# A plan that chooses the engine of low parts and last sums, finer records of Q and K, and column tiles for layer 2 and V in a macaron block

## The chip, the cores and the metric

The kernel runs on one core of one Trainium2 chip. The metric is device time in microseconds (us) of one execution; the time before is the median of three runs. A core has TensorE (PE; its weight loads are shown apart as PEld), VectorE (DVE), ScalarE (ACT), GpSimd (POOL) and SyncE (SP, which here issues most DMAs). They run side by side and meet through semaphores. Every engine takes its own instructions strictly in the order in which the program lists them, so the order in which the kernel is written down decides what waits for what.

## What is computed

A macaron block on x of 32 x 256 x 128 (32 sequences of 256 tokens, width 128): half a feed-forward network, attention, half a feed-forward network, each with a norm in front. The weights of the network are booleans that mean +1 or -1.

```python
def ffn(x, k0, k1, k2, s0, s1, s2):           # 256 -> 512 -> 512 -> 128
    h = concatenate([x, -x], axis=-1)
    h = relu(s0 * (h @ where(k0, 1, -1))) * 2
    h = relu(s1 * (h @ where(k1, 1, -1))) * 2
    return s2 * (h @ where(k2, 1, -1))

def attn(x, Wq, bq, Wk, bk, Wv, bv, gamma, beta):   # 16 heads of 8
    Q, K, V = (heads(x @ W.T + b) for W, b in ((Wq, bq), (Wk, bk), (Wv, bv)))
    a = softmax(einsum('bhqd,bhkd->bhqk', Q, K) / sqrt(8), axis=-1)
    return layernorm(merge(einsum('bhqk,bhkd->bhqd', a, V)) + x, gamma, beta)

x = x + 0.5 * ffn(layernorm(x), ...)
x = x + attn(layernorm(x), ...)
x = x + 0.5 * ffn(layernorm(x), ...)
```

## The kernel before

**Tiling.** Two sequences make a unit: 16 units of 512 tokens, and each unit has two halves (one sequence each) in the attention. Values are split into a high and a low half-precision part, so that two or three half-precision matmuls stand for one in single precision.

**Stages of a unit.** `first(u)` is the first feed-forward network: `normalize` (statistics on DVE, the rest on POOL, or all on DVE where `quick` is set), `turned` (a transpose by DMA from ACT's and POOL's high and low parts, or on PE where `quick` is set), then `ffn`. In `ffn`, layer 0 makes four tiles `p` of 128 x 512, layer 1 four more of eight matmul steps each; `relu_split` takes each tile out of PSUM as a high part (ACT, line 556, `h1h` or `h2h`) and a low part (DVE, line 562, `h1l` or `h2l`). For a hand-picked tile (`SOFT`: the second tile of layer 1) ACT writes the rectified tile a second time (line 559, `full`) and POOL subtracts (line 560). Layer 2 (line 606) makes four groups of 128 tokens, eight steps of 128 columns each. The last sum `x + factor * p` runs on DVE (line 618) for units 0, 1 and 15, and on ACT and POOL (lines 615 and 616) for the others. `norm_attn` and `project` make Q, K and V: `qkhl` (lines 670 and 672), a DMA to DRAM (line 675), and three row DMAs each that lay Q and K out by heads (line 680); V (line 689) is copied into `vaug`. `maxima` computes the scores `nat` once (line 720) for the row maxima `nm` (DVE, line 731); `shift` turns the maxima into extra rows of Q (`mt` at lines 741 and 742, a transpose `pm` at line 748, `mr` at line 753, DMAs at lines 754 and 755); `weigh` computes the scores again (`sc`, line 788), exponentials on ACT (`pt`, line 800) and the context `cx` (line 770). `context` copies and transposes it (`cxT` at line 803, `tp` at line 814), divides (lines 833 and 834), normalizes and adds (lines 836 to 841; on POOL, or on DVE where `quick` is set). `second(u, b)` is the second network; for unit 15 it runs by halves.

**The plan.** Nothing is emitted where it is written. Each `op(...)` notes engine, assumed cost, rank, what it reads and writes, and the buffers it holds. `simulate` then plays the program with these costs: an engine that is free takes the ready operation of lowest rank whose buffers fit; PE may pass over a group that is not ready, within `SKIP` ranks. The order found in this way is the order in which `run` emits each engine's instructions. Scores of the two kinds with the same rank (`kind` "M" and "W") go out interleaved, as they use different row tiles. A unit has 16 ranks; `B0`, `BA`, `BP`, `BW`, `BV` and `B1` shift the stages against one another: the weights of a half come `BW` = 11 ranks after its maxima. `QF` and `QK` say how many first units use the quick norm and PE transposes.

**Tile forms of PE.** A step of `dense` can use the full array ("D", 128*128 in the profile) or four column tiles ("C", 128*32: four weight loads and four matmuls). Scores use row tiles ("R", 32*128), the context column tiles. An operation of kind "F" takes the form that PE is in; after scores it takes the next one in line. Layer 2 and V were always "D", with ranks rounded (`even`) so that they come together.

Of the kernel before, what the change touches and what calls it, by code (L numbers as in the profile page):

```python
# [35 lines left out]
F32 = mybir.dt.float32  # L36
# [7 lines left out]
P = 128  # L44
# [12 lines left out]
QF, QK = 2, 2  # L57

SOFT, SOFT_FIRST, FIRST = ((1, 1),), ((1, 1),), 2
# [5 lines left out]
B0, BA, BP, BW, BV, B1 = -34, -12.911, -7.641, 11, 3, 41.956  # L65

RUSH, AHEAD = 0, 5.808

SKIP0, SKIP, UNTIL = 21.758, 7.907, 11.451

WAIT = 0.087

TURN, DRAIN, SIGNAL = 0.105, 0.22, 0.06

SAME = (0.0, 0.09, 0.09, 0.1, 0.0)
# [18 lines left out]
class _Node:  # L94
    __slots__ = ("n", "eng", "cost", "emit", "rank", "kind", "rows", "lag", "needs", "then", "bufs", "count", "avail", "start", "given", "tiling")


class _Plan:
# [11 lines left out]
    def op(self, eng, cost, emit, r=(), w=(), rank=0.0, kind="D", rows=0, lag=None):  # L110
        x = _Node()
        x.n, x.eng, x.cost, x.emit, x.rank, x.kind, x.rows = len(self.nodes), eng, cost, emit, rank, kind, rows
        x.lag = lag if lag is not None else DRAIN if eng == PE else SIGNAL
        x.then, x.avail, x.start, x.given = [], 0.0, None, lag is not None
# [25 lines left out]
    def simulate(self):  # L140
# [17 lines left out]

        def tiling(x):
            return "R" if x.kind in "WM" else x.tiling if x.kind == "F" else x.kind  # L160

        def begin(group, now):
# [11 lines left out]
            for x in group:  # L174
# [3 lines left out]
                for b in x.bufs:  # L178
# [4 lines left out]
                    if not b.left:  # L183
                        tick += 1
                        heapq.heappush(events, (now + span + x.lag, tick, b.tag))
                for y in x.then:
                    y.avail = max(y.avail, now + span + (x.lag if y.eng != eng or x.given else SAME[eng]))
# [52 lines left out]

        mode = "D"
        while left:
# [8 lines left out]
            while again:  # L251
                again = False
                for eng in range(5):
                    if free[eng] > now + 1e-9 or not ready[eng]:
                        continue
                    if eng == PE:
                        group = choose(now)
                    else:
                        can = [x for x in ready[eng] if x.avail <= now + 1e-9 and fits(x)]
                        group = [min(can, key=lambda x: (x.rank, x.n))] if can else None  # L260
# [31 lines left out]
def tile_macaron(ctx: ExitStack, tc: tile.TileContext, x, Wq, bq, Wk, bk, Wv, bv, gamma, beta, k0, k1, k2, s0, s1, s2, out):  # L292
# [176 lines left out]
    def blanks():  # L469
        for j in range(NV):  # L470
            rank = -500 if j == 0 else (j - 1) * UNIT * 0.5
            op(POOL, 1.35, lambda j=j: nc.gpsimd.memset(vaug[j], 0.0), w=[("V", j)], rank=rank)
            op(POOL, 0.95, lambda j=j: nc.gpsimd.memset(ks[j].bitcast(I32), ONES), w=[("K", j)], rank=rank)
# [9 lines left out]
    def normalize(dst, src, tag, n, rank, scale=1.0, quick=False):  # L483
# [7 lines left out]
        for a in range(0, n, step):  # L491
            part = slice(a, a + step)
            ts = range(a, a + step)
            for t in ts:
# [4 lines left out]
               r=[(mv, t) for t in ts], w=[(ve, a)], rank=rank, lag=0.12)  # L499
            op(POOL, 0.25 + 0.2 * step, lambda part=part: nc.gpsimd.tensor_tensor(rs.t[:, part, 0], ve.t[:, part], nhalf[:, part], ALU.pow),  # L500
               r=[(ve, a), "nhalf"], w=[(rs, a)], rank=rank, lag=0.15)
# [52 lines left out]
    def relu_split(hi, lo, m, ps, w, rank, soft):  # L554

        op(ACT, 0.09 + w / 1280, lambda: nc.scalar.activation(hi.t[:, m, :], ps.t, AF.Relu), r=[ps], w=[(hi, m)], rank=rank)  # L556
        if soft:
            full = buf(work, [P, w], F32, "full", 2, "full")
            op(ACT, 0.09 + w / 1280, lambda: nc.scalar.activation(full.t, ps.t, AF.Relu), r=[ps], w=[full], rank=rank)
            op(POOL, 0.1 + w / 500, lambda: nc.gpsimd.tensor_tensor(lo.t[:, m, :], full.t, hi.t[:, m, :], ALU.subtract), r=[full, (hi, m)], w=[(lo, m)], rank=rank)  # L560
        else:
            op(DVE, 0.08 + w / 985, lambda: nc.vector.scalar_tensor_tensor(lo.t[:, m, :], ps.t, 0.0, hi.t[:, m, :], ALU.max, ALU.subtract),  # L562
               r=[ps, (hi, m)], w=[(lo, m)], rank=rank)

    def ffn(key, srcs, dst, n, rank, span):
# [4 lines left out]
        softs = SOFT_FIRST if key[1] < FIRST and key[0] == "ffn0" else SOFT  # L570

        at = lambda i: rank + span * i / (NF + NF * NF + n)
        even = lambda k: 2 * (k // 2) + 0.9
# [4 lines left out]
        for m in range(NF):  # L578
# [7 lines left out]
            relu_split(*h1, m, ph, w, at(i), (0, m) in softs)  # L586
            i += 1
        for m in range(NF):
# [9 lines left out]
            relu_split(*h2, m, ph, w, at(i), (1, m) in softs)  # L598
        po = psum([P, n, D], f"p3{name}")
        h2s = [(h, m) for h in h2 for m in range(NF)]  # L600
        for t in range(n):

            def layer2(t=t):
                for c in range(NF):
                    for k in range(2):
                        nc.tensor.matmul(po.t[:, t, :], h2[k].t[:, c, bass.ts(t, P)], w2[:, c, :], start=c == 0 and k == 0, stop=c == NF - 1 and k == 1)  # L606

            op(PE, 0.449, layer2, r=[*h2s, "w2"], w=[po], rank=even(at(i)))
# [5 lines left out]
        if 1 < key[1] < NU - 1:  # L614
# [281 lines left out]
```

## Time and profile before

| | us |
|---|---|
| median of three runs (708.55 to 709.5) | 708.56 |
| the profiled execution | 707.94 |
| its span, from the first to the last instruction | 706.1 |
| first row maximum starts | 54.86 |
| last row maximum ends | 658.7 |
| last exponential ends | 675.4 |

A profile shows one execution. A row of the timeline gives the start, the length, the engine, the line, the operation, and the tile written and those read; `x4` means four of them merged into one row, and a bracket at the end says how long the engine had stood idle and who ended it. A row of the waits names who waited for whom, then the total in us, how often, and the longest. A row of the groups ends in the busy time, the mean length in ns and the idle time in front. Matmuls overlap, so the distance from one start to the next tells more of PE than the length of one.

### The profile page before, as it was taken

What the parts mean: (1) busy time and instruction counts of PE and PEld (TensorE: products, weight loads), DVE (VectorE), ACT (ScalarE), POOL (GpSimd) and SP (SyncE); (2) the same over time, 40 slices, a digit from 0 to 9 for tenths busy, and PEclk for the clock granted to TensorE, in tenths of its full rate; (3) what the DMA queues carried; (4) which work ended last, traced back from release to release, by engine and by line L of the source; (5) the groups of instructions that cost most, each with busy time, mean ns of one, the idle gap of its engine ahead of it and who ended that gap; (6) DMA issues with size and microseconds to landing.
All of it is one profiled execution on the core that took longest, in us unless ns stands there. A gap on an engine that the chain in (4) does not pass through costs nothing.

```text
span 706.1 us, 23287 instructions
## 1 busy us (share of the span) xinstructions
PE 652.2 (92%) x9800; PEld 331.8 (47%) x9800; DVE 601.4 (85%) x1229; ACT 527.0 (75%) x770; POOL 445.8 (63%) x579
## 2 busy tenths in 40 slices
PE   2996888999999999999999999999999998989797
PEld 1553343445454454545545454545555454444336
DVE  7789888999989889898989989898988898978564
ACT  3552777878788787888888877888878777867853
POOL 7762647668492877749586956858582928463611
PEclk9998999999999999999999999999999999999989
DMA  5141331422213132232323131332232030410100
GB/s 138 31 120 62 63 107 27 107 42 85 64 33 117 33 108 56 67 81 48 101 44 120 34 108 42 93 56 72 62 48 86 19 117 19 108 33 4 33 1 32
DMA packets 79373, 46.28 MB, mean 66 GB/s; under 512 B 50562, under 2 KB 74628, under 8 KB 79268
## 3 DMA queue, kind: packets, MB, share of 16 engines
q1 hardware_dynamic: 77796, 44.20, 24.7%
q8 instruction: 77, 1.26, 0.7%
q10 hardware_dynamic: 1472, 0.59, 0.3%
q14 instruction: 28, 0.23, 0.1%
HBM read 20.25 MB, written 13.24 MB: 47 GB/s over the span
## 4 chain that ended last, share of the span: by engine, by line
PE 70%; DVE 17%; ACT 6%; issue 3%; DMA 3%; POOL 0%; SPq 0%; ACTq 0%; DVEq 0%; POOLq 0%
PE cx L770 14%; PE p_None L325 12%; PE p L325 9%; PE p L322 7%; PE sc L788 6%; DVE nm L731 6%; PE p L606 4%; ACT pt L800 4%; PE nat L720 3%; PE p_None L606 3%; PE p_None L322 3%; DVE h1l L562 3%; PE tp L814 2%; DMA dm<-mr 1%; PE pq L325 1%
## 5 line engine op out<-in xcount | busy, mean ns | idle before, releaser
L731 DVE TENSOR_REDUCE nm<-nat 128x4 f32<-128x1024 f32 x256 | 310.7, 1217 | 46.9 <-PE nat L720 38.0
L800 ACT ACTIVATE pt<-sc,esc 128x1024 f32<-128x1024 f32 x256 | 284.9, 1116 | 79.7 <-PE nat L720 41.0
L770 PE MATMUL cx<-pt,vaug 128*32 128x256 f32 x2048 | 147.6, 389 | 2.3 <-ACT pt L800 2.3
L325 PEld LDWEIGHTS <-w 128*32 128x32 f16 x3584 | 91.6, 96 | 92.2 <-issue 32.7
L788 PE MATMUL sc<-Q,ks 32*128 32x256 f16 x1024 | 103.6, 275 | 11.0 <-ACT pt L800 8.0
L720 PE MATMUL nat<-ks,Q 32*128 32x256 f16 x1024 | 101.5, 275 | 8.1 <-ACT pt L800 4.1
L770 PEld LDWEIGHTS cx<-pt,vaug 128*32 128x32 f32 x2048 | 64.9, 111 | 54.9 <-issue 16.4
L325 PE MATMUL p_None<-h1h_None,w 128*32 128x512 f16 x780 | 77.4, 382 | 0.2 <-DVE h1l_None L562 0.2
L325 PE MATMUL p_None<-h1l_None,w 128*32 128x512 f16 x780 | 76.8, 379 | 0.0
L325 PE MATMUL p<-h1h,w 128*32 128x512 f16 x644 | 66.2, 383 | 0.4
L788 PEld LDWEIGHTS <-ks 32*128 32x128 f16 x1024 | 31.7, 93 | 73.1 <-issue 64.6
L325 PE MATMUL p<-h1l,w 128*32 128x512 f16 x644 | 65.9, 381 | 0.0
L616 POOL TENSOR_TENSOR x<-x,x 128x512 f32<-128x512 f32 x13 | 16.6, 1279 | 64.8 <-ACT x L615 64.8
L322 PEld LDWEIGHTS <-w 128*128 128x128 f16 x424 | 38.7, 98 | 36.7 <-issue 9.1
L556 ACT ACTIVATE h2h<-p 128x512 f16<-128x512 f32 (+1 forms) x72 | 41.2, 572 | 17.9 <-PE p L322 14.3
L836 POOL TENSOR_TENSOR y<-y,axn 128x256 f32<-128x256 f32 x30 | 21.8, 728 | 49.9 <-DVE y L834 41.3
L556 ACT ACTIVATE h1h<-p 128x512 f16<-128x512 f32 (+1 forms) x72 | 39.4, 571 | 18.2 <-PE p L325 11.1
L720 PEld LDWEIGHTS <-Q 32*128 32x128 f16 x1024 | 31.4, 92 | 38.3 <-issue 35.9
L562 DVE SCALAR_TENSOR_TENSOR h1l<-p,h1h 128x512 f16<-128x512 f32 (+1 forms) x72 | 45.7, 650 | 3.2 <-ACT h1h L556 2.7
L562 DVE SCALAR_TENSOR_TENSOR h2l<-p,h2h 128x512 f16<-128x512 f32 (+1 forms) x54 | 35.3, 653 | 12.0 <-ACT h2h L556 11.8
L562 DVE SCALAR_TENSOR_TENSOR h1l_None<-p_None,h1h_None 128x512 f16<-128x512 f32 x60 | 39.5, 682 | 6.8 <-ACT h1h_None L556 6.6
L322 PE MATMUL p<-h1h,w 128*128 128x512 f16 (+1 forms) x127 | 43.4, 354 | 1.3 <-DVE h1l L562 0.8
(144 smaller groups left out, 1368.4 us busy)
## 6 DMA issues: line engine op xcount, KB each, us to landing
dr<-qkhl SPq DMA_DIRECT2D x32, 256.0 KB
Q<-dr SPq DMA_DIRECT2D x48, 128.0 KB
ks<-dr SPq DMA_DIRECT2D x48, 128.0 KB
x<-in_L_attn_x_dram SPq DMA_DIRECT2D x15, 256.0 KB
out_dram<-x_None SPq DMA_DIRECT2D x15, 256.0 KB
Q<-nought SPq DMA_DIRECT2D x16, 128.0 KB
dm<-mr SPq DMA_DIRECT2D x32, 16.0 KB
Q<-dm SPq DMA_DIRECT2D x32, 16.0 KB
```

What stands on the lines that cost most here:

```text
L322: nc.tensor.matmul(to, w, of, start=start, stop=stop)
L325: nc.tensor.matmul(to[32 * r : 32 * r + 32], w[:, 32 * r : 32 * r + 32], of, start=start, stop=stop)
L556: op(ACT, 0.09 + w / 1280, lambda: nc.scalar.activation(hi.t[:, m, :], ps.t, AF.Relu), r=[ps], w=[(hi, m)], rank=rank)
L562: op(DVE, 0.08 + w / 985, lambda: nc.vector.scalar_tensor_tensor(lo.t[:, m, :], ps.t, 0.0, hi.t[:, m, :], ALU.max, ALU.subtract), r=[ps, ( ...
L606: nc.tensor.matmul(po.t[:, t, :], h2[k].t[:, c, bass.ts(t, P)], w2[:, c, :], start=c == 0 and k == 0, stop=c == NF - 1 and k == 1)
L616: op(POOL, 1.23, lambda: nc.gpsimd.tensor_tensor(dst.t, dst.t, of(), ALU.add), r=reads, w=dsts, rank=at(i))
L720: nc.tensor.matmul(nat.t[:, ii, qc, :], Q.t[32 * r : 32 * r + 32, g, b * S + qc * P : b * S + qc * P + P], K[32 * r : 32 * r + 32, g, b * ...
L731: op(DVE, 1.141, lambda g=g, pr=pr, nat=nat: nc.vector.tensor_reduce(nm.t[:, :, 2 * pr : 2 * pr + 2, g].rearrange("p q i -> p i q"), nat.t ...
L770: nc.tensor.matmul(cx.t[32 * r : 32 * r + 32, g // 2, :], V[:, 2 * b + kc, 4 * (g // 2) + r, 16 * (g % 2) : 16 * (g % 2) + 32], pts[g, r / ...
L788: nc.tensor.matmul(sc.t[:, ii, kc, :], K[32 * r : 32 * r + 32, g, b * S + kc * P : b * S + kc * P + P], Q.t[32 * r : 32 * r + 32, g, b * S ...
L800: op(ACT, 1.012, lambda pt=pt, sc=sc: nc.scalar.activation(pt.t, sc.t, AF.Exp, scale=esc), r=[sc, "esc"], w=[pt], rank=rank - RUSH)
L836: op(e, cost, lambda: eng.tensor_tensor(y.t, y.t, xn.t[:, 2 * b : 2 * b + 2, :], ALU.add), r=[(xn, 2 * b), (xn, 2 * b + 1)], w=[(y, 0)], r ...
```

## The change

- Constants: `QF`, `QK` 2 to 1; a new `QL` = 2; `BW` 11 to 13, `BV` 3 to 4, the other offsets by less than one rank; `RUSH` 0 to 0.302; `SKIP0` 21.758 to 30.226. The hand-picked `SOFT` tiles are gone.
- Lags: the time from an operation's end to its reader's start is now noted by the pair of engines (`AFTER`, `REACH`).
- `relief`: when ACT is free, the plan looks at DVE's ready operations that have an alternative (`alt`: every low part and every last sum). If the detour over ACT and POOL would end no later than `BIAS` after DVE's own end, a new ACT operation is made, and the old one moves to POOL.
- Layer 2 and V become kind "F", and use `dense` and so column tiles where PE is in that form.
- The rows of Q and K are noted apart, so that the plan lets the three row DMAs of one tile overlap.
- The last `QL` units use the quick context and the quick norm of the second network.

```diff
-QF, QK = 2, 2
-
-SOFT, SOFT_FIRST, FIRST = ((1, 1),), ((1, 1),), 2
+QF, QK = 1, 1
+
+QL = 2
...
-B0, BA, BP, BW, BV, B1 = -34, -12.911, -7.641, 11, 3, 41.956
-
-RUSH, AHEAD = 0, 5.808
-
-SKIP0, SKIP, UNTIL = 21.758, 7.907, 11.451
-
-WAIT = 0.087
-
-TURN, DRAIN, SIGNAL = 0.105, 0.22, 0.06
-
-SAME = (0.0, 0.09, 0.09, 0.1, 0.0)
+B0, BA, BP, BW, BV, B1 = -34, -12.145, -7.563, 13, 4, 42.5
+
+RUSH, AHEAD = 0.302, 5.298
+
+SKIP0, SKIP, UNTIL = 30.226, 7.856, 12.452
+
+WAIT = 0.101
+
+KIND2 = 'F'
+
+TURN = 0.1
+
+
+AFTER, REACH = (0.165, 0.085, 0.11, 0.04, 0.0), (0.053, 0.033, 0.037, 0.08, 0.05)
+
+BIAS = 0.471
...
+        def until(x, eng):
+            return x.lag if x.lag is not None else 0.0 if x.eng == eng == PE else AFTER[x.eng] + REACH[eng]
...
+        def relief(now, best):
+
+            nonlocal left
+            for x in sorted((x for x in ready[DVE] if x.alt and x.avail <= now + 1e-9), key=lambda x: (x.rank, x.n)):
+                if best and (best.rank, best.n) < (x.rank, x.n):
+                    return None
+                act, evict, source, temp, pool, rest = x.alt
+                before = sum(y.cost for y in ready[DVE] if y.avail <= now + x.cost and (y.rank, y.n) < (x.rank, x.n))
+                wait = sum(y.cost for y in ready[POOL] if (y.rank, y.n) < (x.rank, x.n))
+                other = max(now + act + 0.2, max(free[POOL], now) + wait) + pool
+                if other > max(free[DVE], now) + before + x.cost + BIAS:
+                    continue
...
+                x.eng, x.cost, x.emit, x.count, x.alt = POOL, pool, rest, 1, None
+                ready[ACT].append(y)
+                left += 1
+                return y
+            return None
...
-                        group = [min(can, key=lambda x: (x.rank, x.n))] if can else None
+                        best = min(can, key=lambda x: (x.rank, x.n)) if can else None
+                        if eng == ACT:
+                            best = relief(now, best) or best
+                        group = [best] if best else None
...
-    def relu_split(hi, lo, m, ps, w, rank, soft):
+    def relu_split(hi, lo, m, ps, w, rank):
...
-        if soft:
...
+        op(DVE, 0.08 + w / 985, lambda: nc.vector.scalar_tensor_tensor(lo.t[:, m, :], ps.t, 0.0, hi.t[:, m, :], ALU.max, ALU.subtract),
+           r=[ps, (hi, m)], w=[(lo, m)], rank=rank,
+           alt=(0.09 + w / 1280, lambda: nc.scalar.activation(full.t, ps.t, AF.Relu), ps, full, 0.1 + w / 500, low(full)))
...
-                        nc.tensor.matmul(po.t[:, t, :], h2[k].t[:, c, bass.ts(t, P)], w2[:, c, :], start=c == 0 and k == 0, stop=c == NF - 1 and k == 1)
-
-            op(PE, 0.449, layer2, r=[*h2s, "w2"], w=[po], rank=even(at(i)))
+                        dense(po.t[:, t, :], h2[k].t[:, c, bass.ts(t, P)], w2[:, c, :], tiling, c == 0 and k == 0, c == NF - 1 and k == 1)
+
+            op(PE, 0.449, layer2, r=[*h2s, "w2"], w=[po], rank=LAYER2(at(i)), kind=KIND2)
...
-        if 1 < key[1] < NU - 1:
-            op(ACT, 0.586, lambda: nc.scalar.activation(dst.t, po.t, AF.Identity, scale=fac), r=[po, "fac"], w=dsts, rank=at(i))
-            op(POOL, 1.23, lambda: nc.gpsimd.tensor_tensor(dst.t, dst.t, of(), ALU.add), r=reads, w=dsts, rank=at(i))
-        else:
...
+        op(DVE, 0.08 + w / 870, lambda: nc.vector.scalar_tensor_tensor(dst.t, po.t, fac, of(), ALU.mult, ALU.add), r=[po, "fac", *reads], w=dsts, rank=at(i),
+           alt=(0.09 + w / 1040, lambda: nc.scalar.activation(dst.t, po.t, AF.Identity, scale=fac), po, dst,
+                0.1 + w / 455, lambda: nc.gpsimd.tensor_tensor(dst.t, dst.t, of(), ALU.add)))
...
-        norm_ffn(("ffn1", u, b), (src, part), n, rank - AHEAD, u == NU - 1)
+        norm_ffn(("ffn1", u, b), (src, part), n, rank - AHEAD, u >= NU - QL)
...
-                op(SP, 0.62, place, r=[dr], w=[("K", j)] if i else [(Q, 0), (Q, 1)], rank=rank, lag=2.2)
+                op(SP, 0.62, place, r=[dr], w=[("K", j, row)] if i else [(Q, 2 + row)], rank=rank, lag=2.2)
...
-        op(PE, 0.672, values, r=[*xTr, "wqkv0", "wqkv1"], w=[pv], rank=2 * ((rank + 2) // 2) + 0.9)
+                    dense(pv.t[:, t, :], xT.t[:, b, bass.ts(t, P)], wqkv[:, 2, a, :], tiling, k == 0, k == 2)
+
+        op(PE, 0.672, values, r=[*xTr, "wqkv0", "wqkv1"], w=[pv], rank=2 * ((rank + 2) // 2) + 0.9, kind=KIND2)
...
+    def rows(Q, b, j):
+        return [(Q, b), *((Q, 2 + row) for row in range(3)), *(("K", j, row) for row in range(4))]
...
-        op(DVE, 0.09, lambda: nc.vector.tensor_scalar(mt.t[:, :, :, 0, :], nm.t, 1.0 / ONE, None, ALU.mult), r=nmr, w=[(mt, 0)], rank=rank)
-        op(DVE, 0.09, lambda: nc.vector.scalar_tensor_tensor(mt.t[:, :, :, 1, :], nm.t, 1.0 / ONE, mt.t[:, :, :, 0, :], ALU.mult, ALU.subtract),
+        op(DVE, 0.2, lambda: nc.vector.tensor_scalar(mt.t[:, :, :, 0, :], nm.t, 1.0 / ONE, None, ALU.mult), r=nmr, w=[(mt, 0)], rank=rank)
+        op(DVE, 0.12, lambda: nc.vector.scalar_tensor_tensor(mt.t[:, :, :, 1, :], nm.t, 1.0 / ONE, mt.t[:, :, :, 0, :], ALU.mult, ALU.subtract),
...
-        if quick:
+        if u == NU - 1:
             x2s[u, b] = x2 = buf(io, [P, 2, D], F32, "x2", NX2, f"x2_{u}_{b}")
...
-            context(u, b, u == NU - 1)
+            context(u, b, u >= NU - QL)
```

## The prediction

> **What bounds the kernel now.** I read the page first, busy times and slices, then three stretches of the windows view, then who waited for whom on TensorE, then the timeline at the start and at the end.
>
> ```profile
> PE 652.2 (92%) x9800; PEld 331.8 (47%) x9800; DVE 601.4 (85%) x1229; ACT 527.0 (75%) x770; POOL 445.8 (63%) x579
> ...
> PEclk9998999999999999999999999999999999999989
> ```
> ```profile
> core 0: us, PE busy (x) PEld busy (x) DVE busy (x) ACT busy (x) POOL busy (x), PEclk, DMA share, GB/s
> 44.00:154.00 110.00, 95.50 (x1278) 46.43 (x1279) 97.16 (x192) 73.31 (x105) 60.75 (x77) 0.95 0.31 77
> 154.00:594.00 440.00, 430.80 (x7060) 220.06 (x7050) 394.95 (x777) 357.43 (x514) 303.51 (x383) 1.00 0.27 69
> 594.00:706.00 112.00, 95.83 (x1294) 49.57 (x1288) 76.21 (x156) 74.39 (x109) 49.10 (x67) 0.97 0.15 36
> ```
> There are three regimes. In the middle PE is busy 430.8 of 440 us (98%), at full clock, so at most 9.2 us of plain idleness can be won there. Early, DVE is busy 97.2 of 110 us and PE is 14.5 us idle. Late, PE is 16.2 us idle and no engine is full: a chain of latencies. The chain of waits agrees: PE 70%, DVE 17%, ACT 6%. What ended PE's idle time in the middle:
> ```profile
> PE pm L748 <- DVE mt L742: 4.6, 8, 1.0
> PE sc L788 <- DMA Q<-dm: 2.9, 3, 1.2
> ```
> That is 7.5 us of the 9.2: eleven waits of about a microsecond on the path from the maxima to the shifted Q.
>
> The sum is made against the profiled execution: span 706.1, its own time 707.94, so 1.84 us lie around the span. The median of the runs is 708.56, 0.6 above; I add that at the end.
>
> **The start.** The first maximum runs at 54.86, its matmul at 54.08, though the last row of Q and K for unit 0 was issued at 49.37 and took 0.60 to issue. A Q row written from DRAM (Q<-dm) lands 1.98 us after its issue in the chain of waits, which puts the data at about 51.95. What stands between is unit 1 on its quick path: its transposes (50.46) and its Q and K products (52.62 to 54.08). With QF and QK at 1, unit 1's two transposes go by DMA instead. DVE loses four fxn (1.24 us together), four axn (1.17) and two xT subtractions (0.68, 0.69), 3.8 us; GpSimd gains six tensor ops, 2 x (1.04 + 1.04 + 1.16) = 6.5, inside a stretch where it is 55% busy (60.75 of 110); ACT swaps a 0.58 cast for a 0.62 one. SP gains two DMA transposes at 1.24 us of queue each, and they can come ahead of unit 0's rows, as one does now at 46.15. The rows of Q and K being apart in the record takes nothing off the chip by itself: SP already issued three Q rows and three K rows from 44.21 to 49.37 without waiting between them; only the plan thought that the rows of one tile follow each other 2.2 us apart, so it can now place the first scores earlier. Bounds: -3.8 (all of the DVE time was in the chain) to +2.5 (two transposes ahead of the rows). I take **-1.5**, three quarters of the 2.1 us between landing and use.
>
> **The early stretch.** Of PE's waits from 55 to 154 us, nm ended 3.6, qkhl 2.4, mt 1.6 and h1l 0.2: 7.8 us by DVE. The rule called relief moves a low part or a sum when the detour ends no later than 0.471 us after DVE would. The rows of such a move:
>
> ```profile
> L562 DVE SCALAR_TENSOR_TENSOR h1l<-p,h1h 128x512 f16<-128x512 f32 x64 | 42.7, 679 | 2.5 <-ACT h1h L556 2.1
> ...
> L560 POOL TENSOR_TENSOR h2l<-full,h2h 128x512 f16<-128x512 f32 x16 | 18.5, 1155 | 1.4 <-ACT full L559 1.4
> ...
> L559 ACT ACTIVATE full<-p 128x512 f32<-128x512 f32 x16 | 9.6, 598 | 0.0
> ```
> 0.68 us off DVE for 0.60 on ACT and 1.16 on GpSimd. By the plan's own costs the detour is 0.49 + 0.2 + 1.12 = 1.81 against 0.60 + 0.47, so it needs 0.74 us of other DVE work in front: one maximum (1.22 us a row) is enough if GpSimd is free. Bounds 0 to -7.8; I take **-2**, a quarter, because most waits there are for maxima, which no rule moves, and the fixed detours of before (33 low parts, 26 sums: 33 x 0.68 + 26 x 0.75 = 42 us of DVE) are given up first.
>
> **The middle.** Weights trail maxima by 13 ranks instead of 11 (BW). A unit takes 16 ranks and 39.26 us (three units repeat in 117.77 us in the chain), a rank 2.45, so the path nm, mt, pm, dm, Q has 4.9 us more; the three waits for Q<-dm (2.9 us) should go. The waits of pm for mt stay in part: the plan now gives mt 0.2 + 0.12 instead of 0.09 + 0.09, so pm is placed later, but this is what makes mt late:
>
> ```profile
> 292.05 1.27 POOL L616 TENSOR_TENSOR x_None<-x_None,x 128x512 f32<-128x512 f32 x1
> ```
> ```profile
> 292.14 1.23 DVE L742 SCALAR_TENSOR_TENSOR mt<-nm,mt 128x32 f16<-128x32 f32 x1
> ```
> A 0.19 us operation (its median) took 1.23 while GpSimd held on, and pm started at 293.43. More work on GpSimd makes more such meetings; I count half, 2.3 of the 4.6. The third part is layer 2 and V. Counted in the timeline from 154 to 594 us, PE changes 38 times directly between column tiles and the full array; such a change costs 0.095 us (0.311 from the last 512-column start to the next start, 0.216 of it stream): 3.6 us. The 22 transposes tp stay full-array, so at least some 16 changes can go, 1.5 us. Leaving for the row tiles of the scores costs the same 0.1 from either form. That makes 2.9 + 2.3 + 1.5 = 6.7; against it stand new waits that I can't place: every low part moved to GpSimd holds it for 1.16 us, and one meeting like the one above costs 1 us. With one or two of them counted I take **-5**; bounds -9.2 - 3.6 = -12.8 (all idleness and all changes gone) and +5 (as much lost as won).
>
> What the columns cost is the unknown. 1024 + 192 steps of 128 columns become four each, with four weight loads of 32 columns. No row shows four such loads in one step; the nearest is pm, one column tile with two 128-column steps, against layer 2 now:
>
> ```profile
> 353.49 0.22 PE L748 MATMUL pm<-ident,mt 128*32 128x128 f16 x1
> ...
> 353.55 0.22 PE L748 MATMUL pm<-ident,mt 128*32 128x128 f16 x1
> ...
> 370.45 0.22 PE L606 MATMUL p_None<-w,h2h_None 128*128 128x128 f16 x1
> 370.51 0.22 PE L606 MATMUL p_None<-w,h2l_None 128*128 128x128 f16 x1
> ```
> 57 ns against 55.5 a step, each with its load: x 1216 that is +1.8 us. The other end is a step as long as one load's own record, 96 ns: (96 - 55.5) x 1216 = +49. I take 0, near the first, since a 32-column load was followed by its matmul 55 ns later in that very row, and the eight loads at the head of a column phase start within 25 ns of each other.
>
> [...]
>
> **The end.** This is the largest term that one can see:
>
> ```profile
> 649.09 0.65 PE L814 MATMUL tp<-ident,cxT 128*128 128x128 f32 x4
> ...
> 672.63 0.62 PE L325 MATMUL p_None<-xT_None,w 128*32 128x512 f16 x4
> ...
> 679.21 0.55 PE L814 MATMUL tp<-ident,cxT 128*128 128x128 f32 x3
> ...
> 690.06 0.49 PE L322 MATMUL p<-xT,w 128*128 128x256 f16 x3
> ```
> Unit 14 takes 23.5 us from its last context transpose to the first matmul of its second FFN, through GpSimd and a DMA transpose; unit 15, on DVE, takes 10.9. With QL = 2 unit 14 goes the second way and its FFN can start some 11 us sooner, in a stretch (658 to 679) where PE idles and falls to half clock (0.84 in the 22 us from 660). Now the whole of unit 14's FFN and unit 15's first half are still in PE's order when the last half is ready: its first layer waits until 690.06 behind unit 14's layer 2, its second layer until 697.62 behind the other half. Three pieces: the last half is not queued behind the other (its layer 0 starts 694.90, xT was done at 693.08): -1.8; DVE no longer puts three h2l (0.66 each) and a z that took 1.45 instead of 0.60 into the last chain: -2.8; and the gap between the last two halves of exponentials (662.6 to 665.5), which is the shift's latency with only 3 weights left to cover it, is covered by 5 with BW = 13: -2.3, less 2 more unpaired weights at 0.5 us of PE, +1. Sum -5.9; DVE pays for unit 14 by unit 15's rows: two halves of four ops at 0.42 and two z at 0.30, four fxn at 0.30 and one xT at 0.69, 6.5 us, in a stretch where it is 68% busy. I take **-5.5**, bounds -11 (unit 14's whole lead) and 0.
>
> **Sum:** -1.5 - 2 - 5 - 5.5 = -14. 707.9 - 14 = 693.9, and with 0.6 to the median **694.5 us**.
>
> **Rivals.** (a) *Columns paced by their weight loads*, slower: layer 2 and V steps take 66 to 96 ns. It decides from 14 us / 1216 = 11.5 ns a step; half of the way to 96 ns gives 694.5 + 25 = 719. For it: no row shows four loads in 55 ns. Against: pm. 7%. (b) *GpSimd becomes late*, slower: it is 69% busy in the middle (303.5 of 440); 60 more low parts at 1.16 would be 70 us, 85%, and the context and the norms for the second FFN queue behind them in one order, while the room from context to that FFN is 42.5 - 5.3 - 29 = 8.2 ranks, 20 us, against 9.1 ranks before. Each unit whose FFN comes late by more than 14 / 14 = 1 us turns the sum; 2 us a unit give 694.5 + 28 = 722, 1.5 us 715. For it: the 23.5 us of unit 14 are already longer than the room. Against: PE may take other groups within 7.9 ranks. 16%. (c) *Little comes of it*: PE in the middle is full anyway, relief seldom fires and DVE takes back its 42 us, the end keeps its order; the start and half of the end, 3 to 5 us, remain less what DVE loses: 704 to 709. 11%. The forecast has 66%.
>
> **How the numbers follow.** A measurement tells about 0.2%, 1.4 us. The forecast's own range is 684 to 703: all terms near half of their distance to the lower bounds (-24), or a third of them won (-5). Below 684 lie 5%; (a) and (b) reach upward, and 716 leaves out some 13%. So 683 to 716. Faster: 66 plus half of (c), 71%; same: 4% from (c); slower: 25%.
>
> **What would show it.** Right: the first maximum before 54; no PE wait for Q<-dm in the middle; layer 2 on 128*32 with four steps in 55 to 58 ns; unit 14's second FFN starting within 14 us of its transposes; more than 33 rows of the subtraction on GpSimd. Wrong: layer 2's step over 66 ns, PE waiting for xT or GpSimd's hl in the middle, or DVE above 95% there.

## The result and the profile after

| | before | after |
|---|---|---|
| median, us | 709.03 (708.55 to 709.76, 4 runs) | 699.28 (697.69 to 700.56, 4 runs) |
| ratio of the runs | | 0.9861, 95% interval 0.9835 to 0.9886 |
| profiled execution, us | 707.94 | 698.52 |
| its span, us | 706.1 | 696.7 |

The change makes the kernel 1.4% faster, 9.7 us by the medians. The first line of busy times of the changed kernel, then its windows view in the three stretches of the prediction (columns: the stretch and its length, busy time of each engine with its instructions, granted clock, DMA share, GB/s):

```profile
PE 648.1 (93%) x13033; PEld 326.6 (47%) x13033; DVE 598.9 (86%) x1224; ACT 531.4 (76%) x782; POOL 453.7 (65%) x580
```
```profile
44.00:154.00 110.00, 99.37 (x1922) 48.15 (x1920) 96.72 (x194) 81.76 (x124) 82.05 (x97) 1.00 0.34 83
154.00:594.00 440.00, 432.09 (x9590) 218.72 (x9589) 395.00 (x761) 361.76 (x523) 310.75 (x388) 1.00 0.30 71
594.00:696.00 102.00, 88.29 (x1372) 45.51 (x1370) 78.20 (x169) 68.26 (x99) 28.31 (x44) 0.97 0.12 29
```
The middle has not changed: PE 432.1 of 440 us against 430.8, DVE 395.0 against 395.0. The early stretch is denser (PE 99.4 of 110 against 95.5), and the late one is shorter.

To see where the time came from, I cut the span at events that both programs have: the first row maximum of units 0, 4, 8 and 14 (the maxima run in the same order in every kernel), and the end.

| us | first maximum | to unit 4 | to unit 8 | to unit 14 | to the end |
|---|---|---|---|---|---|
| before | 54.9 | 139.7 | 158.8 | 234.9 | 117.9 |
| after | 51.3 | 137.9 | 155.0 | 237.3 | 115.2 |

That is -3.5 at the start, -1.8 to unit 4, -3.7 to unit 8, +2.4 from there to unit 14, and -2.8 at the end, together the 9.4 us of the spans. These are two single executions. How far such stages drift by themselves shows in the kernel with one quick unit (below): it runs the same matmuls in the same order as the changed one past unit 14, and reaches unit 14's first maximum 5.1 us later. A difference of 2 us in one stage is therefore no proof of a cause.

The waits view of the changed kernel from 154 to 594 us, TensorE only (who waited for whom: total us, times, longest), answers to the two lines of the prediction:

```profile
PE pm L795 <- DVE mt L789: 1.3, 4, 0.5
PE p L371 <- issue: 1.0, 1, 1.0
PE sc L835 <- ACT pt L847: 0.9, 2, 0.6
PE pm L795 <- DVE h1l L608: 0.8, 2, 0.5
```
The wait for `Q<-dm` (2.9 us before) is gone and the one for `mt` fell from 4.6 to 1.3, as the prediction had it. In their place stand short waits for low parts (`h1l`), for exponentials and "issue". I also counted every gap of PE's matmul stream in this stretch from the trace's records (no view prints this count), with a 512-column step taken as 216 ns and a 128-column one as 55.7: 52.2 us before, 50.2 after. Waits for `Q<-dm` fell by 3.4 us and those for `mt` by 3.5, direct changes between column tiles and full array by 1.3 (38 to 25 of them); waits for DVE's low parts of the network (`h1l`, `h2l`) rose by 2.7, "issue" by 2.0, `qkhl` by 1.0, `nm` and `pt` by 0.7 or so each. Work per microsecond in the middle stayed what it was.

The start, in SyncE's timeline of the changed kernel (start, length, engine, line, operation, tiles):

```profile
44.71 1.87 SPq L724 DMA_DIRECT2D Q<-dr  x3
46.68 1.84 SPq L724 DMA_DIRECT2D ks<-dr  x3
48.61 1.27 SPq L577 DMA_TRANSPOSE xT<-hl  x1
```
Three rows of Q and three of K go out in one piece, and the transpose for unit 1 comes behind them. In the kernel before an input load and a transpose stood between them:

```profile
44.21 0.57 SPq L680 DMA_DIRECT2D Q<-dr  x1
...
46.15 1.25 SPq L531 DMA_TRANSPOSE xT<-hl  x1
...
49.37 0.60 SPq L680 DMA_DIRECT2D ks<-dr  x1
```
The first score runs at 50.90 instead of 54.08.

The end, in TensorE's timeline of the changed kernel:

```profile
648.13 0.66 PE L861 MATMUL tp<-ident,cxT 128*128 128x128 f32 x4
...
662.27 0.61 PE L371 MATMUL p_None<-xT_None,w 128*32 128x512 f16 x8
...
671.51 0.66 PE L861 MATMUL tp<-ident,cxT 128*128 128x128 f32 x4
...
685.61 0.60 PE L368 MATMUL p<-xT,w 128*128 128x256 f16 x4
```
Unit 14 now takes 14.1 us from its last context transpose (648.13) to its second network (662.27), against 23.5 before. The last half's context transpose comes at 671.51, 2.1 us behind the last exponential (3.8 before), and its network starts 14.1 us later at 685.61 (15.7 before, 679.21 to 694.90); from there to the end it is some 11 us in both.

What the planner gave away, in the groups view of the changed kernel (busy us, mean ns of one, then idle time before it):

```profile
L610 ACT ACTIVATE full<-p_None 128x512 f32<-128x512 f32 x30 | 18.4, 614 | 0.0
L789 DVE SCALAR_TENSOR_TENSOR mt<-nm,mt 128x32 f16<-128x32 f32 x32 | 16.5, 516 | 0.3
```
The second of these in the kernel before:

```profile
L742 DVE SCALAR_TENSOR_TENSOR mt<-nm,mt 128x32 f16<-128x32 f32 x32 | 11.1, 348 | 0.4
```
With the 26 of `full<-p` and one of half the width that makes 57 low parts on ScalarE and GpSimd against 33 before, while more last sums are back on DVE (14 are given away against 26). DVE's total hardly moved, 601.4 to 598.9 us. What changed is when it does which.

The granted clock differs too. Its records are at half for 17 us of the kernel before (62.0 to 68.8, 102.9 to 106.3 and 669.5 to 676.4 us) and for 6.8 us of the changed one (631.9 to 638.7). By the matmul steps that ran in these stretches I estimate that the half clock added at most 7.3 us of streaming before and 3.3 us after; how much of that ended on the path was not separated.

### The profile page after: what moved, and what is told of

It reads as the page before. It is cut to its first block, busy times and chain, and to the rows that moved or that the text cites. A ratio compares the mean times of both kernels' runs of the same rounds, so it can differ in the third digit from the quotient of the medians.

```text
span 696.7 us, 29746 instructions
## 1 busy us (share of the span) xinstructions
PE 648.1 (93%) x13033; PEld 326.6 (47%) x13033; DVE 598.9 (86%) x1224; ACT 531.4 (76%) x782; POOL 453.7 (65%) x580
## 3 DMA queue, kind: packets, MB, share of 16 engines
q8 instruction: 102, 1.67, 1.0%
## 4 chain that ended last, share of the span: by engine, by line
PE 69%; DVE 18%; ACT 5%; DMA 4%; issue 3%; SPq 1%; POOL 1%; ACTq 0%
PE p_None L371 15%; PE p L371 15%; PE cx L817 14%; DVE nm L778 8%; PE sc L835 7%; PE p L368 6%; PE p_None L368 4%; ACT pt L847 3%; PE nat L767 2%; DMA x<-in_L_attn_x_dram 2%; PE tp L861 2%; PE pq L371 2%; DVE mt L789 1%; PE pv L371 1%; DVE h1l L608 1%
## 5 line engine op out<-in xcount | busy, mean ns | idle before, releaser
L371 PEld LDWEIGHTS <-w 128*32 128x32 f16 x3808 | 93.8, 96 | 89.8 <-issue 32.7
L835 PE MATMUL sc<-Q,ks 32*128 32x256 f16 x1024 | 105.1, 274 | 11.6 <-ACT pt L847 11.5
L817 PEld LDWEIGHTS cx<-pt,vaug 128*32 128x32 f32 x2048 | 63.5, 110 | 51.1 <-issue 13.5
L371 PE MATMUL p<-h1h,w 128*32 128x512 f16 x792 | 80.3, 382 | 0.0
L371 PE MATMUL p<-h1l,w 128*32 128x512 f16 x792 | 79.6, 379 | 0.0
L371 PE MATMUL p_None<-h1h_None,w 128*32 128x512 f16 x712 | 71.2, 382 | 0.2
L371 PE MATMUL p_None<-h1l_None,w 128*32 128x512 f16 x712 | 70.7, 379 | 0.0
L608 DVE SCALAR_TENSOR_TENSOR h2l<-p,h2h 128x512 f16<-128x512 f32 (+1 forms) x64 | 41.8, 653 | 15.7 <-ACT h2h L607 15.4
L368 PEld LDWEIGHTS <-w 128*128 128x128 f16 x368 | 34.6, 99 | 37.2 <-issue 11.9
L607 ACT ACTIVATE h2h_None<-p_None 128x512 f16<-128x512 f32 x60 | 35.8, 597 | 10.6 <-PE p_None L368 7.5
L608 DVE SCALAR_TENSOR_TENSOR h2l_None<-p_None,h2h_None 128x512 f16<-128x512 f32 x47 | 32.1, 682 | 7.0 <-ACT h2h_None L607 6.9
L371 PE MATMUL p_None<-xT_None,w 128*32 128x512 f16 x480 | 34.9, 389 | 2.6 <-DMA xT_None<-hl_None 1.7
L542 DVE BATCH_NORM_STATS2 st_f<-x 128x6 f32<-128x128 f32 x128 | 31.3, 273 | 6.7 <-DMA x<-in_L_attn_x_dram 6.5
```

The costliest lines, as they stand in the source:

```text
L368: nc.tensor.matmul(to, w, of, start=start, stop=stop)
L371: nc.tensor.matmul(to[32 * r : 32 * r + 32], w[:, 32 * r : 32 * r + 32], of, start=start, stop=stop)
L542: op(DVE, 0.195, lambda t=t, st=st: nc.vector.bn_stats(st.t, of()[:, t, :]), r=[srcs[t // 2]], w=[st], rank=rank)
L817: nc.tensor.matmul(cx.t[32 * r : 32 * r + 32, g // 2, :], V[:, 2 * b + kc, 4 * (g // 2) + r, 16 * (g % 2) : 16 * (g % 2) + 32], pts[g, r / ...
L835: nc.tensor.matmul(sc.t[:, ii, kc, :], K[32 * r : 32 * r + 32, g, b * S + kc * P : b * S + kc * P + P], Q.t[32 * r : 32 * r + 32, g, b * S ...
```

## The experiments

Twelve kernels ran beside the kernel before, four on one chip at a time. Ratios are against the kernel before on the same chip; spans and stages are those of the one profiled execution.

| kernel | median us | ratio (95%) | span | first max. | to unit 4 | to unit 8 | to unit 14 | to the end |
|---|---|---|---|---|---|---|---|---|
| a_nudge | 701.88 | 0.9889 (0.9835 to 0.9942) | 697.5 | 50.9 | 137.9 | 156.1 | 238.8 | 113.8 |
| a_layer2_full | 704.76 | 0.9934 (0.9905 to 0.9964) | 699.7 | 51.4 | 139.0 | 159.8 | 235.3 | 114.3 |
| a_ql1 | 705.02 | 0.9942 (0.9904 to 0.9980) | 703.2 | 53.7 | 138.7 | 155.4 | 238.8 | 116.5 |
| a_ql3 | 703.64 | 0.9939 (0.9908 to 0.9970) | 698.9 | 51.2 | 136.2 | 155.8 | 238.3 | 117.4 |
| a_q22 | 704.77 | 0.9936 (0.9906 to 0.9967) | 703.3 | 53.0 | 139.1 | 155.0 | 239.5 | 116.8 |
| a_bw11 | 734.24 | 1.0359 (1.0302 to 1.0417) | 729.5 | 52.2 | 150.9 | 167.7 | 241.5 | 117.1 |
| a_rows_joined | 711.75 | 1.0063 (1.0039 to 1.0086) | 711.3 | 56.6 | 139.7 | 160.7 | 235.7 | 118.7 |
| a_relief_off | 724.17 | 1.0212 (1.0159 to 1.0265) | 721.5 | 51.6 | 143.5 | 164.2 | 242.5 | 119.7 |
| a_fixed_detours | 715.01 | 1.0086 (1.0051 to 1.0122) | 711.8 | 52.6 | 143.5 | 159.5 | 239.7 | 116.6 |
| a_fixed_as_many | 713.09 | 1.0077 (1.0050 to 1.0104) | 712.8 | 54.2 | 141.6 | 161.6 | 238.2 | 117.2 |
| b_relief | 710.07 | 1.0035 (1.0012 to 1.0059) | 708.2 | 56.8 | 141.4 | 156.4 | 236.2 | 117.4 |
| b_ql2 | 707.59 | 0.9973 (0.9947 to 0.9999) | 707.8 | 58.3 | 140.4 | 158.5 | 234.8 | 115.9 |

Names with `a_` are the changed kernel with one part undone, those with `b_` the kernel before with one part added. First maxima differ by up to some 3 us for a reason that is not the program's: how soon TensorE's clock comes to full (from 17.6 to 26.6 us), which the last section shows.

### Layer 2 and V on the whole array

```diff
-KIND2 = 'F'
+KIND2 = 'D'
```


> Layer 2 and V go back to the full array with rounded ranks, the rest as in the changed kernel (699.3). Theory: the column form saves some 15 direct changes of 0.095 us and gives about as much back in steps (59.0 us per thousand on average against 57.6), so 699 to 701, the same within a plan's noise. Rival: the column form frees the order and carries the gain, then 704 or more. Rival 2: the column steps cost, then 696 or less.

0.9934 against 0.9861: about 0.7%, 5 us, which is the first rival's side (704 or more) and not the theory's. The column form does not cost anything here. The run also rounds the ranks of layer 2 again, so the number is for both. In the profiles it is 2.9 us: 1.1 are lost up to unit 4 and 4.7 between units 4 and 8, and 2.9 come back behind them. That the column form frees the order fits this, but no stage shows it.

### Weights 11 ranks behind the maxima

```diff
-B0, BA, BP, BW, BV, B1 = -34, -12.145, -7.563, 13, 4, 42.5
+B0, BA, BP, BW, BV, B1 = -34, -12.145, -7.563, 11, 3, 42.5
```


> BW 13 to 11 and BV 4 to 3, the rest as in the changed kernel (699.3). Theory: the waits for Q<-dm come back in the middle (3.4 us) and the gap between the last two halves of exponentials at the end (2.9 us), so 703 to 706. Rival: the middle is bound by PE and the waits only move, so 698 to 701.

734.24, far outside both. The waits view of this kernel from 154 to 594 us shows a part of it:

```profile
PE sc L835 <- DMA Q<-dm: 9.8, 7, 3.8
```
The wait that cost 2.9 us in the kernel before and nothing in the changed one costs 9.8 here, 13.5 over the whole span. The profiled span is 32.7 us longer than the changed kernel's, so over half of the loss is elsewhere: in the waits view the waits for `pt` add some 6 us, the granted clock is at half for 17 us instead of 6.8, and the rest has no name. At the end the gap between the last two halves of exponentials is back at 2.8 us, and the last half starts 81.0 us after unit 14's first maximum instead of 77.2. The two extra ranks hide the shifted Q, and the rest of the new order needs them more than the old one did.

### One quick unit at the end, and three

```diff
-QL = 2
+QL = 1
```


> QL 2 to 1: unit 14's context and second norm go over GpSimd and the DMA transpose again, the rest as in the changed kernel (699.3). Theory: the end loses what it won after 638 us, 4 to 7 us: 703 to 706. Rival: PE has other work there and the last half's own chain sets the end, so 698 to 701.

0.9942. By the medians the second quick unit is worth 0.8%, as the theory said. The trace asks for caution: on TensorE this kernel runs the same 12,377 matmuls in the same order as the changed one until 643.8 us, and is already 5.5 us late at 602.9, before anything that differs. Of the 6.5 us between the two spans, 1.0 is more than what it was already late there. Of these 5.5 us 2.4 come from a clock that reaches full later at the start, and 1.5 arise where this execution's clock is at half (80.6 to 84.0 us) and the changed kernel's is not. The part's own worth lies between 1 and 5.7 us.

```diff
-QL = 2
+QL = 3
```


> The changed kernel with its last three units quick instead of two. In the changed kernel the lead over the kernel before is given back between 594 and 638 us, where TensorE waits for exponentials and for a transpose by DMA. Theory (the detour by GpSimd and DMA of unit 13 is what is late there): 695 to 698 us, ratio 0.981 to 0.985. Rival (the quick unit's extra work on TensorE and VectorE costs as much in the middle as it saves): 699 to 704 us.

0.9939, not below the changed kernel: the number is in the rival's range, and the theory's gain did not come. The ten executions reach from 698.6 to 708.3 us. In the profiled one (700.67, one of the fastest) the end is longer (117.4 against 115.2); whether the middle pays for it, as the rival had it, one profile does not tell.

### The first two units quick, as before

```diff
-QF, QK = 1, 1
+QF, QK = 2, 2
```


> QF and QK 1 to 2: unit 1 on the quick path again, the rest as in the changed kernel (699.3). Theory: the first maximum goes back from 51.3 to some 54 us, and the time by 2 to 3.5 us: 701 to 703. Rival: the early lead is given back before 638 us anyway, so 698 to 700 with the first maximum at 54.

0.9936, about 0.75% worse than the changed kernel, more than the theory's size, and not by its mechanism. The first maximum is at 53.0 instead of 51.3, but the quick unit 1 does not put it there: SyncE's first row already goes out 1.6 us later (46.28 against 44.71), in a profile whose clock is full only from 23.8 us instead of 20.9, and from that row to the first score it takes 6.2 us in both. Over the ten kernels with split rows the first row goes out the later, the later the clock is full (44.3 us at 19.9, 47.6 at 26.6), and 46.3 at 23.8 lies between. Where the rest is lost no single stage shows.

### The rows of one tile joined in the record

```diff
-w=[("K", j, row)] if i else [(Q, 2 + row)]
+w=[("K", j, r) for r in range(4)] if i else [(Q, r) for r in range(5)]
```


> The changed kernel with the row copies of one tile of Q and K following each other in the record again, as before; all else as changed. The prediction gave the split rows the waits for Q (2.9 us in the middle) and a part of the start (1.5 us): by it 702 to 705 us, ratio 0.990 to 0.995. Rival (the wait for Q went because the planner places the work otherwise): 698 to 701 us.

711.75, 2.0% worse than the changed kernel; both numbers were too small. SyncE's timeline of this kernel at the start:

```profile
46.33 0.57 SPq L724 DMA_DIRECT2D Q<-dr  x1
...
48.00 0.48 SPq L591 DMA_DIRECT2D x<-in_L_attn_x_dram  x1
48.68 1.25 SPq L577 DMA_TRANSPOSE xT<-hl  x1
49.98 0.59 SPq L724 DMA_DIRECT2D Q<-dr  x1
...
51.90 0.60 SPq L724 DMA_DIRECT2D ks<-dr  x1
```
The load and the transpose are back between the first and the second row: since the plan believes that a row has to land before the next one of its tile goes, it fills the queue with other issues meanwhile, and on the chip the rows queue behind them. From the first row's issue to the first score it takes 9.8 us here (46.33 to 56.13), 9.9 in the kernel before (44.21 to 54.08) and 6.2 in the changed one (44.71 to 50.90). In all fourteen kernels this distance goes by the rows alone: 5.9 to 6.5 us in the ten with split rows, whether one unit or two are quick, and 9.8 to 10.4 in the four with joined rows. So the split rows are the gain at the start. Beyond it, 5.6 us are lost between units 4 and 8; the waits for `mt` there and before are 4.2 us from the first maximum to unit 8, against 1.3 in the changed kernel.

### The planner's choice

Off, so that DVE keeps every low part and sum:

```diff
-best = relief(now, best) or best
+best = best
```


> The changed kernel with the relief switched off: VectorE makes every low part and every last sum, also those that the kernel before put on ScalarE and GpSimd at fixed places (33 low parts and 26 sums). Theory (VectorE's low parts are the wait that took the place of those removed, so taking them off it pays): some 56 low parts and 14 sums go back to an engine that is busy 395 of 440 us in the middle, at 0.2 to 0.5 us each some 15 to 25 us of work, of which a third or more ends on the path: 706 to 716 us. Rival (VectorE has room, the relief only shuffles): 698 to 702 us.

724.17, worse than the theory's range. The waits view of this kernel from 154 to 594 us names its sign, behind 3.5 us of "issue":

```profile
PE p_None L371 <- DVE h1l L608: 3.3, 5, 0.7
PE p L371 <- DVE h1l L608: 2.6, 4, 0.7
PE p_None L371 <- DVE h1l_None L608: 2.2, 4, 0.6
...
PE p L371 <- DVE h1l_None L608: 1.6, 5, 0.3
```
9.7 us of waits for low parts, against 1.2 in the changed kernel for the same readers. DVE's busy time rises by 30 us, from 598.9 to 628.9, more than the 15 to 25 us of the theory.

With the fixed places of before in its stead (the second tile of layer 1 always, the sums of units 2 to 14):

```diff
+            relu_split(*h2, m, ph, w, at(i), m == 1)
...
+        if 1 < key[1] < NU - 1:
+            op(ACT, 0.586, lambda: nc.scalar.activation(dst.t, po.t, AF.Identity, scale=fac), r=[po, "fac"], w=dsts, rank=at(i))
+            op(POOL, 1.23, lambda: nc.gpsimd.tensor_tensor(dst.t, dst.t, of(), ALU.add), r=reads, w=dsts, rank=at(i))
```


> The changed kernel with the low parts and sums given away at the fixed places of the kernel before in place of the planner's choice; columns, split rows and quick last units stay. Theory of the prediction (the planner's choice is a small part of the gain, the waits it removes come back elsewhere): 699 to 703 us, ratio 0.986 to 0.991. Rival (the planner's choice is what pays): 704 to 709 us, ratio 0.993 or more.

715.01: the rival's side, and beyond its number. All other parts of the change together, with the old detours, make the kernel 0.9% slower than before.

With as much given away as the planner gives, at fixed places:

```diff
+            relu_split(*h1, m, ph, w, at(i), m == 1 and key[0] == 'ffn1')
...
+            relu_split(*h2, m, ph, w, at(i), m == 1)
...
+        if 1 < key[1] < 9:
```


> The changed kernel with as much given away as the planner gives, but at fixed places: 50 low parts (the second tile of layer 1 always, that of layer 0 in every second FFN) and 14 sums (units 2 to 8) against the planner's 56 and 14. Theory A (what pays is that VectorE has less to do): 699 to 704 us, ratio 0.986 to 0.993. Theory B (what pays is when it is given away): 708 to 716 us, ratio 0.999 to 1.010, like the fixed detours of before.

713.09, inside theory B: about as much work taken off DVE, at places that don't follow its load, brings nothing over the old detours (1.0077 against 1.0086). It is a fair match: 50 low parts against 57, 14 sums in both, and DVE busy for 598.8 us against 598.9. With the changed kernel's constants, then, it matters which operations are taken off DVE, and not only how many. That it is the lateness of DVE which picks the right ones is how the rule is made; no other set of fixed places was tried, and no constants fitted to them.

### One part added to the kernel before

The planner's choice alone (`relief` and the alternatives, `BIAS` 0.471, as in the diff of the change), and the second quick unit alone:

```diff
-context(u, b, u == NU - 1)
+context(u, b, u >= NU - 2)
```


> The kernel before with the planner's choice of low parts and sums put in place of its fixed detours, nothing else of the change (its own constants, layer 2 and V on the whole array, joined record, one quick unit). Fixed detours in the changed kernel cost 16 us against the planner's choice, so: theory A (the choice is worth as much by itself) 693 to 700 us, ratio 0.978 to 0.988; theory B (choice, columns and constants pay only together, since the planner then knows when VectorE will be late) 703 to 710 us, ratio 0.992 to 1.002.

> The kernel before with its last two units quick instead of one, nothing else of the change. Theory (each part pays by itself; quick units gave about 5.7 us of the changed kernel when taken away): 702 to 706 us, ratio 0.990 to 0.996. Rival (the quick second unit pays only once the other parts have freed PE and VectorE at the end): 707 to 712 us.

1.0035 and 0.9973: the choice alone makes the kernel before slightly slower, at the end of theory B's range, and the quick unit gives a quarter of a per cent, so the rival holds there too. The same choice that is worth 2.2% when taken out of the changed kernel is worth nothing when put into the old one.

### Is it one lucky order?

```diff
-WAIT = 0.101
+WAIT = 0.1
...
-BIAS = 0.471
+BIAS = 0.45
```


> The changed kernel with two of the planner's constants moved by a hair (BIAS .471 to .45, WAIT .101 to .1), so that the same parts are planned in a slightly other order. If the parts of the change make the gain, the ratio to the kernel before stays within 0.4% of the changed kernel's 0.986: 0.982 to 0.990, 697 to 702 us. If the gain is mostly the luck of one order, it leaves that band by more than 0.4%, up or down, and the single-part runs so far (each about 0.7 to 0.8% worse) would be no more than that luck.

0.9889, inside the band. It is one nudge, and it moved little: by the names in the trace DVE and GpSimd run all their instructions in the same order in both, and TensorE's order first differs at 89.7 us. So it shows that the gain is not a knife's edge, not that all orders near it are as good. Its interval, 0.9835 to 0.9942, also holds the ratios of the four kernels at 0.9934 to 0.9942. That each of those changes costs 0.7 to 0.8% by itself, and not by the luck of an order, is thus not shown; the larger losses (11 ranks, joined rows, no choice, fixed places) lie far outside.

**What follows from all of them.** Undone one at a time with the other constants kept, six parts cost 0.7, 5.0, 0.8, 0.75, 2.0 and 2.2%; together that is 11.5%, eight times the change's 1.4%. So none of these numbers is a part's share. Each holds the part's own worth and what the new offsets lose without it. The reading that fits both sets of runs, argued and not tested, is that the offsets (13 and 4 ranks, `WAIT`, `SKIP`) suit only an order in which rows, choice and columns are all present. It was not tried to fit the offsets again for each part, so how much of a number is the part and how much the misfit stays open. No run beats the changed kernel.

## Why the prediction was right, and where it was not

The direction and the place (start and end) were right, and 699.28 lies 4.8 us above the forecast. Term by term, the profiled spans fell by 9.4 us, not 14:

**Start, -1.5 predicted, -3.5 measured.** The prediction had two causes in one term: unit 1's quick work, which stands between the landing of the rows and their use, and the plan's belief that the rows of one tile follow each other. The first is refuted by a_q22, where unit 1 is quick again and the first score still comes 6.2 us after the first row. The second is what paid. From the last row's issue to the first score it now takes 3.0 us instead of 4.7; that is -1.7, near the predicted -1.5. Missing was the time between the rows: SyncE did not issue the six "without waiting between them". An input load and a transpose issue of 1.25 us stood between, put there by the plan's belief. Without them the last row goes out 3.2 us behind the first instead of 5.2, another -2.0.

**Early stretch, -2 predicted, -1.8 measured to unit 4.** The size is right. The half that was not expected to move did: waits for maxima (3.6 us before) fell to 0.6 us in the waits from 44 to 154 us, and the one for `qkhl` from 2.4 to 0.2. "A quarter, because most waits there are for maxima, which no rule moves" overlooked, as I read it, that a low part taken off DVE lets the next maximum start earlier. But DVE need not be the only cause: the kernel before had 10.2 us of half clock in this stretch and the changed one none, by the steps in it up to 4 us of streaming. What stayed is the waiting for exponentials, 5.7 us before and 4.7 after in that stretch.

**Middle, -5 predicted, -1.3 measured from unit 4 to unit 14.** This is the step that failed. Over these ten units the changed kernel and a_ql1, with the same matmuls in the same order, differ by 1.8 us, so the -1.3 is hardly told from nothing, but it is far from -5. Each of its three removals came true: no wait for `Q<-dm`, `mt` down by more than half, 38 direct changes of form down to 25. The allowance for what would take their place, "one or two" meetings of DVE and GpSimd, was too small: by the count of gaps 7 us of new waits stand against 8 us of old ones. `mt` itself was held longer by GpSimd, its mean rising from 348 to 516 ns, as the prediction feared: 16 of the 32 took more than 0.3 us, 10 before, and every one of these ends 0.04 to 0.05 us after a GpSimd instruction. Its readers were placed later and waited less all the same. DVE is 395.0 us busy in the middle before and after. With two engines at 98% and 90%, a wait that is removed seems to uncover the next one; no run tests this by itself.

**End, -5.5 predicted, -2.8 measured from unit 14's first maximum.** Unit 14's lead came nearly as priced (23.5 to 14.1 us, where the prediction asked for 14), and the last exponential's end to the end of the span went from 30.7 to 27.4 us, -3.3 of the predicted -4.6 (-1.8 and -2.8). Its pieces lie elsewhere: 1.7 before the last context transpose, 1.2 from there to the transposes `t`, and only 0.4 from the queue: the last half's layer 0 still stands 1.4 us behind other work once its `xT` is done (684.23 to 685.61), where it stood 1.8 before. The piece that failed is the gap between the last two halves of exponentials, -2.3. It closed, from 2.9 to 0.2 us, but not by an earlier last half. Counted from unit 14's first maximum, the last half's exponentials start at 77.3 before and 77.2 after, while the half before them ends at 74.4 and 77.0. Against the kernel before, the 13 ranks moved other work into the gap and did not shorten what ends last.

**Rivals.** (a) Columns paced by weight loads: a step of four tiles takes 56.0 ns in the median (lines in the last section), 55.5 before; the rival is refuted. In the trace the four loads of a step start within 0.02 us of each other and take 97 ns each (they start from 123.449 to 123.469 us in one step), so they overlap. (b) GpSimd late: it is busy 310.8 us of the middle against 303.5, since twelve fewer sums pay for over half of the 24 additional low parts; no PE wait for it is in the list. (c) Little comes of it: its 704 to 709 us are excluded by the interval, but what it said of the middle, that PE is full there anyway, came nearer than the forecast.

## What to carry to other kernels

Where a planner orders the work, a noted dependency that the hardware does not have (here between the rows of one tile, three of which go out in 1.87 us) costs twice: the wait it imagines (1.7 us here), and the real work it slips into the imagined gap (2.0). When work is taken off an engine that is nearly full, the amount is not all that counts: taken at fixed places it brought 1.3% here against taking nothing, and by the planner's choice another 2.2%, but that only together with the changed kernel's constants. And a part's worth is measured in both directions, taken out of the new kernel and put into the old one: where the two disagree as here (2.2% and -0.35%), the parts and the constants fitted to them are one change.

## What the hardware showed unexpectedly

**TensorE's first microseconds are a matter of the execution.** Two timelines of TensorE around 22 us, the same instructions in the same order, first the changed kernel, then the one with one quick unit:

```profile
22.13 0.38 PE L368 MATMUL p<-h1l,w 128*128 128x512 f16 x1
22.34 0.38 PE L368 MATMUL p<-h1h,w 128*128 128x512 f16 x1
```
```profile
23.17 0.63 PE L368 MATMUL p<-h1l,w 128*128 128x512 f16 x1
23.59 0.63 PE L368 MATMUL p<-h1h,w 128*128 128x512 f16 x1
```
A step of 512 columns takes 216 ns in the one and 427 in the other, half the pace, until about 25.7 us. The trace's records of the granted clock say the same: the first, at full, begins at 20.9 us in the one and at 26.0 in the other. (The windows view reads 1.00 for both from 18 to 26 us, as it takes time without a record as full.) This alone puts the second kernel 2.4 us behind. The first full clock comes late, at 23.8 to 26.6 us, in the profiles of a_q22, a_rows_joined, a_fixed_as_many, b_relief and b_ql2 too; it comes at 17.6 in that of before. By SyncE's first row these kernels are 1.6 to 3.4 us behind the changed kernel or the kernel before, and their first maxima are to be read with that taken off. In the profiles of the kernel before and the changed one every finished stretch of full or half clock lasts a whole number of times 3.413 us: 3.413 or 6.827 at half, 30.720 to 610.986 at full. What sets when the clock comes to full was not shown.

**Stalls in dense column steps.** TensorE's timeline of the changed kernel in layer 2 of an early unit, each row four column tiles of one step:

```profile
123.56 0.24 PE L371 MATMUL p<-w,h2h 128*32 128x128 f16 x4
123.61 0.24 PE L371 MATMUL p<-w,h2l 128*32 128x128 f16 x4
124.93 0.24 PE L371 MATMUL p<-w,h2h 128*32 128x128 f16 x4 [1.08 <-issue]
```
Steps follow at 56 ns, then TensorE stands for 1.3 us, with 1.08 of it put down to "issue", and goes on. It happens twice in such steps (again at 168.5), after some 270 and 320 instructions of TensorE (matmuls and weight loads) in 3 us; the kernel before never has more than 128 in 3 us and never stalls so. Density alone does not do it: in the 3 us up to 66.9 us 371 instructions pass without such a stall, and the kernel with one quick unit, with the same matmuls in the same order there, stalls only at the second place. The instruction packets grew from 1.26 to 1.67 MB with the change; whether the stalls come from that, or from what else, was not shown.
